# Layer 3's exponentials as a quotient of Sigmoids, and layer 2's h in the order (batch, node)

## The chip, the cores and the metric

The kernel runs on one core of a Trainium2 chip. The core has a matrix engine (TensorE, "PE" in the profile, with "PEld" for its weight loads), a vector engine (VectorE, "DVE"), a scalar engine for functions of one variable (ScalarE, "ACT"), a general engine (GpSimd, "POOL") and a queue for transfers (SyncE, "SP"). They run side by side and wait for each other with semaphores. The metric is the device time of one execution in microseconds (us).

## The reference, cut to what matters

The input x is (128 graphs, 64 nodes, 256 features), fp32, with one 64 x 64 adjacency matrix. Four layers follow one another, each as x = layernorm(x + layer(x)). Layers 0 and 1 (a graph convolution with batch norms, and an attention with an MLP) aren't touched by the change. Layer 2 is two graph convolutions, then four rounds of LSTMs over windows of p nodes; layer 3 is an attention of a graph with itself.

```python
# layer 2, after its convolutions: h is (batch, node, 256)
for p in range(1, 5):
    nw = T // p
    wins = h[:, :nw * p, :].reshape(B * nw, p, H)
    last = lstm_last(Wih[p-1], Whh[p-1], bih[p-1], bhh[p-1], wins)   # p steps over each window
    h = h.at[:, arange(nw) * p + (p - 1), :].set(last.reshape(B, nw, H))

# layer 3
Wh = einsum('bnf,fo->bno', h, W)
e = (Wh @ a1)[:, :, None] + (Wh @ a2)[:, None, :]
e = where(e >= 0, e, 0.2 * e)
e = where(adj == 0, -inf, e)
h_prime = einsum('bij,bjo->bio', softmax(e, -1), Wh)
```

So each round p reads the nodes 0, p, 2p ... as step 0, the nodes 1, p+1, ... as step 1, and so on, and overwrites the last node of each window.

## The kernel before, in words

**Tiles and blocks.** The 128 graphs are cut into 16 blocks of 8 graphs (512 rows of 256 features, four tiles of 128 rows) and into 4 groups of 32 graphs. Work tiles (`mem`) and PSUM tiles (`PS`) are handed out from stocks. Layer 2's h of a group is one SBUF tile `Hg[g]`, features on the partitions, 4096 floats each; `hT[g]` is its view as (partition, half of the features c, node n, graph b). With b last, the 32 graphs of one node are neighbours in memory.

**Order of the work.** Each piece of work is a generator that yields a `step` with an engine and an estimated duration before it issues instructions. `flow` keeps an estimated clock per engine and always continues the generator that could start soonest, so the order of instructions on each engine is fixed when the program is built and follows from the estimates in the `step` calls. A step for ScalarE may name its function table (`tbl="exp"`, `"sigmoid"`, `"gelu"`): a change of table adds 1.3 us to the estimate.

**Layer 2.** `gcn_block` runs the convolutions of one block and the LSTM of p=1, whose result is written into h through `hT_block(i)` (L1357). `unit` runs the windows of p = 2, 3 or 4 over one group: p=2 and p=3 in two units per group (16 and 16, or 12 and 9 windows, times 32 graphs), p=4 in one unit per group for three groups (16 windows, 32 graphs), and in two units of 16 graphs for the last group. `src` is the part of h that a unit reads, `x_of(s, q)` its step s, `out_of` writes the new h (L1389). A unit of 32 graphs is cut into two halves q: by windows where the count of windows is even, by graphs otherwise.

In `lstm`, the gates of step 0 are products with h as the moving operand (L1055). Later steps of a unit in halves take seven products for eight (sums and differences of halves and weights): T1 = x_v - x_u on POOL (L1147), T3 = h_v - x_v on VectorE (L1173), and the products go through `product` (L1127), of which one per gate, A11, has the half x_u of h as its moving operand. The last two units, in one part, use `plain_steps`: products with h (L1264) and with the hidden state (L1266).

**Layer 3.** `last_block(i, t0, nt)` handles a block (the last four blocks in two halves of two tiles). It loads the residual x, copies its part of h to a work tile in the order (graph, node) on ScalarE (L1467), transposes it on TensorE (`to_tm`, L359), adds (L1478), normalises, transposes again (L353), multiplies with W and the two score columns (L1507), builds the scores in PSUM (L1531, L1532), caps and leaks them (L1536, L1538), takes the row maximum (L1539), negates it (L1540), takes one Exp per tile with the sum as a by-product (L1544), divides (L1546, L1547), transposes (L1553), multiplies with Wh (L1563), adds to x (L1574), normalises (L272 to L314) and stores (L1578). The blocks of groups 0 to 2 begin as soon as the last unit of their group has ended; so layer 3's blocks run among the LSTMs of later groups, whose Sigmoids and tanhs are on ScalarE too (L1203 to L1286).

Of the kernel before, what the change touches and what calls it, by code (L numbers as in the profile page):

```python
# [10 lines left out]
AF = mybir.ActivationFunctionType  # L11
ALU = mybir.AluOpType
AX = mybir.AxisListType
PSUM = bass.MemoryType.PSUM

P = 128
B, N, D = 128, 64, 256
# [16 lines left out]
def kernel(ctx: ExitStack, tc: tile.TileContext, a: dict, out: bass.AP):  # L34
    nc = tc.nc
    V, S, G, T = nc.vector, nc.scalar, nc.gpsimd, nc.tensor

    def bc_mid(ap, n):

        return ap.unsqueeze(1).to_broadcast([ap.shape[0], n, ap.shape[1]])  # L40

    def bc_last(ap, n):

        return ap.unsqueeze(2).to_broadcast([ap.shape[0], ap.shape[1], n])

    def tm(s):

        return s.rearrange("p (t d) -> p t d", t=NT)

    def fm(s):  # L50

        return s.rearrange("p (c k) -> p c k", c=2)
# [59 lines left out]
    def mark(*key):  # L112
        done[key] = Clock.end
# [7 lines left out]
    def step(e, us, ps=0, sl=0, waits=True, at=None, tbl=None):  # L121

        return (e, us, ps, sl, waits, at, tbl)
# [83 lines left out]
    def ctile(shape, name, pool=cp):  # L212
        return pool.tile(shape, F32, tag=name, name=name)
# [6 lines left out]
    Hg = [ctile([P, 4 * NT * D], f"h{g}", big) for g in range(NG)]  # L220
    Hs = [Hg[i // 4][:, (i % 4) * NT * D : (i % 4 + 1) * NT * D] for i in range(NBLK)]
    H = [fm(s) for s in Hs]
    hT = [t.rearrange("p (c n b) -> p c n b", c=2, n=N) for t in Hg]
    XD = [dram.tile([P, NT, D], F32, tag=f"xd{i}", name=f"xd{i}") for i in range(NBLK)]

    PS = Stock([ctile([P, NT * D], f"ps{j}", psp) for j in range(4)])
    mem = Stock([ctile([P, NT * D], f"t{j}", big) for j in range(TEMPS)])
# [96 lines left out]
    def joined(ps, n=2 * NT):  # L324

        return ps.rearrange("p (s g e) -> p g s e", s=2, e=N)[:, :n]

    def runs(ap):

        if len(ap.shape) == 2:  # L330
            return ap.rearrange("p (g s e) -> p g s e", s=2, e=N)
        return ap.rearrange("p t (c s e) -> p (t c) s e", s=2, e=N)

    def aggregate(ps, y, mT):


        for c in range(2):
            for t in range(NT):
                for f, to in enumerate(halves):
                    for s, h in enumerate(halves):  # L340
                        T.matmul(  # L341
                            part(ps, s, c * NT + t)[to],
                            y[h, t, c * P + f * N : c * P + (f + 1) * N],
                            mT[h, h],
                            start=True,
                            stop=True,
                        )
# [7 lines left out]
    def to_tm(ps, yT):  # L355

        for t in range(ps.shape[1]):
            for c in range(2):
                T.transpose(ps[:, t, c * P : (c + 1) * P], yT[:, c, t * P : (t + 1) * P], ident)  # L359
# [13 lines left out]
    def mm_tm(ps, yT, w, nk):  # L373

        for t in range(NT):
            for k in range(nk):
                T.matmul(  # L377
                    ps[:, t, :],
                    yT[:, k, t * P : (t + 1) * P],
                    w[:, k, :],  # L380
                    start=(k == 0),
                    stop=(k == nk - 1),
                )

    def by_chunk(ap):
        return ap.rearrange("(k p) m -> p k m", p=P)
# [19 lines left out]
    with c0:  # L406
# [299 lines left out]
        for k, w in zip(("Wc", "Wq", "Wk", "Wv", "Wo", "W1", "W2"), (Wc, Wq, Wk, Wv, Wo, W1, W2)):  # L706
            src = by_chunk(a[f"L1_gnn_{k}"])
# [312 lines left out]

    def hT_block(i):

        return hT[i // 4][:, :, :, (i % 4) * 8 : (i % 4) * 8 + 8]

    def lstm(p, n, parts, x_of, out_of):

# [279 lines left out]
    def gcn_block(i):  # L1306
        yield step("T", 1.15, ps=1, sl=1)
        ps = PS.take()
        s_a = mem.take()
        aggregate(PS[ps], X[i], bdAT)  # L1310
        yield step("Q", 4.0, waits=False)
        nc.sync.dma_start(XD[i], X[i])
        mem.add([Xs[i]], Clock.end, part=("x", i // 2) if i < 8 else None)
        mark("x", i)
        yield step("S", 1.05, ps=-1)
        S.copy(runs(mem[s_a]), joined(PS[ps]))
        PS.give(ps)
        yield step("T", 3.45, ps=1, sl=1)
        ps = PS.take()
        s_h1 = mem.take()  # L1320
        mm_tm(tm(PS[ps]), fm(mem[s_a]), Wg0, 2)
        mem.give(s_a)
        yield step("V", 1.25, ps=-1)
        h1 = tm(mem[s_h1])
        V.tensor_tensor(h1, tm(PS[ps]), bc_mid(rb0, NT), ALU.add)
        PS.give(ps)
        yield step("S", 1.05)
        S.activation(mem[s_h1], mem[s_h1], AF.Relu)
        yield step("T", 1.15, ps=1, sl=1)
        ps = PS.take()  # L1330
        s_a = mem.take()
        aggregate(PS[ps], h1, bdAT)
        mem.give(s_h1)
        yield step("S", 1.05, ps=-1)
        S.copy(runs(mem[s_a]), joined(PS[ps]))
        PS.give(ps)
        yield step("T", 3.45, ps=1, sl=1)
        ps = PS.take()
        s_h2 = mem.take()
        mm_fm(fm(PS[ps]), Wg1, fm(mem[s_a]), 2)  # L1340
        mem.give(s_a)
        yield step("V", 1.4, ps=-1)
        h2 = fm(mem[s_h2])
        for c in range(2):
            V.tensor_tensor(
                h2[:, c, :].rearrange("p (b n) -> p b n", b=8),
                fm(PS[ps])[:, c, :].rearrange("p (b n) -> p b n", b=8),
                bc_mid(rb1[:, c, :], 8),
                ALU.add,
            )  # L1350
        PS.give(ps)
        t = yield step("S", 1.05)
        S.activation(mem[s_h2], mem[s_h2], AF.Relu)  # L1353


        def out_of(q, c, o, th):
            V.tensor_tensor(  # L1357
                hT_block(i)[:, c, :, :].rearrange("p n b -> p b n"), o, th, ALU.mult
            )

        yield step("T", 0.0)
        h2 = h2.rearrange("p c (b n) -> p c b n", b=8)
        yield from lstm(1, TB, [(slice(0, TB), 8)], lambda s, q: h2, out_of)
        yield step("V", 0.0)
        mem.give(s_h2)
        mark("p", 1, i)

    def unit(p, g, w0, nw, b0, nb):
        src = hT[g][:, :, w0 * p : (w0 + nw) * p, b0 : b0 + nb].rearrange("p c (w q) b -> p c w q b", q=p)

        hn = nw * nb // 2
        even = nw % 2 == 0
        parts = [(slice(q * hn, (q + 1) * hn), nw // 2 if even else nw) for q in range(2)]
        if nb < BG:
            parts = [(slice(0, 2 * hn), nw)]

        def half(ap, q):

            if len(parts) == 1:
                return ap  # L1380
            if even:
                return ap[..., q * nw // 2 : (q + 1) * nw // 2, :]
            return ap[..., q * nb // 2 : (q + 1) * nb // 2]

        def x_of(s, q):
            return half(src[:, :, :, s, :], q)

        def out_of(q, c, o, th):
            V.tensor_tensor(half(src[:, c, :, p - 1, :], q), o, th, ALU.mult)  # L1389

        yield from lstm(p, nw * nb, parts, x_of, out_of)
        mark("p", p, g, w0, nw, b0, nb)
# [63 lines left out]
    def last_block(i, t0=0, nt=NT):  # L1456
# [3 lines left out]
        x = tm(mem[s_x])[:, :nt, :]  # L1460
        nc.sync.dma_start(x, XD[i][:, t0 : t0 + nt, :])
        r = nt / NT
        yield step("S", 2.2 * r, sl=1)
        s_h = mem.take()
        hb = fm(mem[s_h])[:, :, : nt * P]
        for c in range(2):
            S.copy(  # L1467
                hb[:, c, :].rearrange("p (b n) -> p b n", n=N),
                hT_block(i)[:, c, :, 2 * t0 : 2 * (t0 + nt)].rearrange("p n b -> p b n"),
            )  # L1470
        yield step("T", 0.9 * r, ps=1)
        ps = PS.take()
        px = tm(PS[ps])[:, :nt, :]
        to_tm(px, hb)
        mem.give(s_h)
        mark("read", i)
        yield step("V", 0.1 + 1.2 * r, ps=-1)
        V.tensor_tensor(x, px, x, ALU.add)  # L1478
# [6 lines left out]
        px = fm(PS[ps])[:, :, : nt * P]  # L1485
# [40 lines left out]
        e, aT, d = (mem[s_e][:, j * nt * N : (j + 1) * nt * N].rearrange("p (t m) -> p t m", t=nt) for j in range(3))  # L1526
# [8 lines left out]
        mx = sm.tile([P, NT], F32, tag="mx3", name="mx3")  # L1535
# [1 line left out]
        PS.give(ps)  # L1537
        V.scalar_tensor_tensor(e, e, 0.2, e, ALU.mult, ALU.max)  # L1538
        V.reduce_max(mx[:, :nt], e, axis=AX.X)  # L1539
        V.tensor_scalar(mx[:, :nt], mx[:, :nt], -1.0, None, ALU.mult)  # L1540
        yield step("S", 0.3 * nt, tbl="exp")
        sums = sm.tile([P, NT], F32, tag="sums3", name="sums3")
        for t in range(nt):
            S.activation(e[:, t, :], e[:, t, :], AF.Exp, bias=mx[:, t : t + 1], accum_out=sums[:, t : t + 1])  # L1544
        yield step("V", 0.3 + 0.3 * r)
        V.reciprocal(sums[:, :nt], sums[:, :nt])  # L1546
        V.tensor_tensor(e, e, bc_last(sums[:, :nt], N), ALU.mult)  # L1547
        yield step("T", 0.1 + 0.5 * r, ps=1)
# [36 lines left out]
    seq, n = [], 0  # L1585
# [85 lines left out]
    def last_of(i, *part):  # L1671
        return (lambda: ready(("wx",), *units_at_end(i)), lambda: last_block(i, *part), 3)
# [66 lines left out]
```

## Time and profile before

| what | value |
|---|---|
| median of 3 runs | 2407.23 us (2405.26 to 2409.41) |
| profiled execution, its own time | 2409.44 us |
| its span in the profile | 2407.7 us |
| busy: PE, DVE, ACT, POOL | 2287.2, 1287.7, 1187.4, 591.7 us |
| granted TensorE clock, mean | 0.982 |
| layer 2's units (L1127 with h) | from about 1340 us |
| layer 3's first copy (L1467) | 1859.6 us |
| last write of h (L1389) | 2372.1 us |

Busy time is the time in which an engine worked on an instruction; matmuls are pipelined, so the mean length of one is more than the distance from one to the next. In a group line, the columns after the bar are busy time in us, mean length of one in ns, and then the idle time of the engine just before these instructions with what ended it. A matmul's name lists the moving operand first and the stationary one second; a tile goes by the name of the memory that it lies in, so "x", "t", "wA" or "rows" can be a work tile in lent memory.

### The profile page before, as it was taken

Reading aid. Unit: us, or ns where it says so; the run is one execution under the profiler, and the core shown is the slowest. Engines: PE = TensorE matmul, PEld = TensorE weight load, DVE = VectorE, ACT = ScalarE, POOL = GpSimd, SP = SyncE. Lnnn points to the kernel's source line nnn. Section 1 sums busy time; section 2 is a strip of 40 time slices with the busy share of each in tenths; the row PEclk is TensorE's granted clock in tenths of the full one; section 3 lists DMA queues with packets and bytes.
Section 4 is the critical chain, followed back from the end, with each engine's and each line's share of the span. In section 5 each row is a group of like instructions: output and inputs, shape, how many; then the busy total and the mean of one; then the engine's idle time right before and its main releaser. Section 6 shows DMA issues by size and latency. Waiting matters only on the chain.

```text
span 2407.7 us, 40603 instructions
## 1 busy us (share of the span) xinstructions
PE 2287.2 (95%) x16916; PEld 1759.9 (73%) x16916; DVE 1287.7 (53%) x2904; ACT 1187.4 (49%) x2189; POOL 591.7 (25%) x441
## 2 busy tenths in 40 slices
PE   8999788999989999999999999999999999998997
PEld 4548665666665666666667788899999888887785
DVE  4557678566483474744643433454444444455546
ACT  2257643544434544335453443444444653468766
POOL 0012134232242232331321222222221222122122
PEclk9999899999999999999999999999999999999998
DMA  6100301000000000001000000000001000001111
GB/s 162 49 1 1 111 23 49 28 10 10 1 12 17 10 10 10 1 10 36 36 19 27 18 1 1 17 2 1 1 1 36 1 10 9 19 27 66 40 36 45
DMA packets 42633, 57.91 MB, mean 24 GB/s; under 512 B 6224, under 2 KB 35536, under 8 KB 42448
## 3 DMA queue, kind: packets, MB, share of 16 engines
q1 hardware_dynamic: 41344, 54.22, 7.0%
q8 instruction: 133, 2.18, 0.4%
q10 hardware_dynamic: 1104, 1.08, 0.1%
q14 instruction: 52, 0.43, 0.1%
HBM read 38.52 MB, written 16.78 MB: 23 GB/s over the span
## 4 chain that ended last, share of the span: by engine, by line
PE 60%; DVE 16%; ACT 7%; POOL 3%; issue 2%; POOLq 0%; ACTq 0%; DVEq 0%
PE ps L1127 26%; PE ps L1055 11%; PE ps L365 7%; PE ps L377 4%; PE ps L938 4%; DVE ln_st L272 3%; ACT x L314 2%; PE ps L808 2%; POOL ln_rs L308 1%; PE ps L1507 1%; DVE x L300 1%; PE ps L341 1%; DVE ln_mv L273 1%; PE ps L353 1%; DVE ln_nm L311 1%
## 5 line engine op out<-in xcount | busy, mean ns | idle before, releaser
L1127 PE MATMUL ps<-x,x 128*128 128x256 f32 x928 | 225.0, 380 | 0.7 <-DVE t L1195 0.7
L1127 PEld LDWEIGHTS ps<-x,x 128*128 128x128 f32 x928 | 173.5, 190 | 24.9 <-issue 1.6
L314 ACT ACTIVATE x<-x,ln_nm,ln_rs 128x256 f32<-128x256 f32 x212 | 112.3, 592 | 133.3 <-DVE ln_nm L311 131.9
L1127 PE MATMUL ps<-t,x 128*128 128x256 f32 x672 | 163.7, 380 | 0.0
L1127 PEld LDWEIGHTS ps<-t,x 128*128 128x128 f32 x672 | 126.4, 190 | 17.1 <-DVE x L1195 0.8
L308 POOL TENSOR_TENSOR ln_rs<-ln_rs,neghalf 128x4 f32<-128x4 f32 (+1 forms) x72 | 71.2, 990 | 212.0 <-DVE ln_rs L274 186.4
L365 PE MATMUL ps<-t,W1T 128*128 128x512 f32 x256 | 117.8, 607 | 0.0
L1055 PE MATMUL ps<-h,wL 128*128 128x192 f32 (+2 forms) x480 | 103.9, 371 | 4.8 <-ACT h L1353 4.8
L272 DVE BATCH_NORM_STATS2 ln_st<-x 128x6 f32<-128x256 f32 x260 | 99.7, 403 | 0.4
L1055 PEld LDWEIGHTS ps<-h,wL 128*128 128x128 f32 x480 | 75.6, 192 | 29.9 <-issue 22.5
L294 POOL TENSOR_TENSOR ln_rs<-ln_rs,neghalf 128x4 f32<-128x4 f32 x32 | 36.9, 1153 | 217.1 <-DVE ln_rs L274 217.0
L1055 PE MATMUL ps<-h,x 128*128 128x256 f32 x384 | 86.7, 380 | 2.2 <-ACT t L1067 1.8
L1067 ACT ACTIVATE t<-ps,bih 128x512 f32<-128x512 f32 (+3 forms) x98 | 57.2, 634 | 55.8 <-PE ps L1055 55.1
L1203 ACT ACTIVATE x<-x,bih 128x512 f32<-128x512 f32 (+2 forms) x69 | 44.6, 648 | 80.3 <-DVE x L1193 80.0
L1186 DVE COPY x<-ps 128x256 f32<-128x256 f32 (+2 forms) x69 | 26.1, 378 | 108.4 <-PE ps L1127 107.6
L365 PEld LDWEIGHTS ps<-t,W1T 128*128 128x128 f32 x256 | 47.6, 195 | 49.6 <-issue 49.5
L365 PE MATMUL ps<-t,wA 128*128 128x512 f32 x160 | 76.8, 626 | 5.5 <-ACT t L784 5.5
L1055 PEld LDWEIGHTS ps<-h,x 128*128 128x128 f32 x384 | 72.6, 190 | 12.9 <-ACT t L1067 2.2
L1186 DVE COPY t<-ps 128x256 f32<-128x256 f32 (+2 forms) x51 | 18.8, 373 | 103.8 <-PE ps L1127 103.5
L1067 ACT ACTIVATE x<-ps,bih 128x512 f32<-128x512 f32 (+3 forms) x86 | 51.5, 650 | 40.6 <-PE ps L1055 40.4
L273 DVE BATCH_NORM_AGGREGATE ln_mv<-ln_st 128x2 f32<-128x6 f32 x448 | 71.3, 167 | 0.0
L1193 DVE TENSOR_TENSOR x<-ps,x 128x512 f32<-128x512 f32 (+2 forms) x69 | 41.4, 602 | 53.0 <-PE ps L1127 43.6
(714 smaller groups left out, 5713.2 us busy)
## 6 DMA issues: line engine op xcount, KB each, us to landing
t<-in_x_dram SPq DMA_DIRECT2D x26, 512.0 KB, 4.3
xd<-x SPq DMA_DIRECT2D x16, 512.0 KB, 2.6
x<-xd SPq DMA_DIRECT2D x8, 512.0 KB, 3.3
out_dram<-x SPq DMA_DIRECT2D x8, 512.0 KB, 2.9
h<-in_x_dram SPq DMA_DIRECT2D x5, 512.0 KB, 5.2
wL<-in_L_gnn_Wih_dram SPq DMA_DIRECT2D x2, 1024.0 KB, 5.0
x<-in_L_gnn_Whh_dram SPq DMA_DIRECT2D x2, 1024.0 KB, 5.4
x<-xd SPq DMA_DIRECT2D x5, 256.0 KB, 2.9
```

Source lines behind the costliest of these rows:

```text
L272: V.bn_stats(st[:, t, :], y[:, t, :])
L273: V.bn_aggr(mv[:, t, :], st[:, t, :])
L308: G.tensor_tensor(rs, rs, neghalf[:, :n], ALU.pow)
L314: S.activation(y[:, t, :], y[:, t, :], AF.Identity, scale=rs[:, t : t + 1], bias=nm[:, t : t + 1])
L365: T.matmul(ps[:, c, :], w[:, k, (off + c) * P : (off + c + 1) * P], yT[:, k, :], start=(k == 0), stop=(k == nk - 1),)
L377: T.matmul(ps[:, t, :], yT[:, k, t * P : (t + 1) * P], w[:, k, :], start=(k == 0), stop=(k == nk - 1),)
L808: T.matmul(pv[r * N : (r + 1) * N, b, :, :], x1T[:, k, b * N : (b + 1) * N], Wv_par[:, k, r, :, :], start=(k == 0), stop=(k == 1),)
L938: T.matmul(tm(PS[ps])[:, t, :], fm(mem[gs[k // 2]])[:, k % 2, t * P : (t + 1) * P], W2[:, k, :], start=(k == 0), stop=(k == 3),)
L1055: T.matmul(spread(fm(PS[ps])[:, j, :n], q), WL[p][0][:, k, m], x_of(0, q)[:, k], start=(k == 0), stop=(k == 1),)
L1067: S.activation(of(sl)[:, j], fm(PS[ps])[:, j, :n], AF.Tanh if g == 2 else AF.Sigmoid, bias=bias(g, c))
L1127: T.matmul(dst, WS[p][name](k, g), y[:, k], start=first and k == 0, stop=k == 1, skip_group_check=not first)
L1186: V.tensor_copy(y[:, 1, :], v[:, 0, :])
```

## The change

`hT` becomes (partition, c, graph b, node n): the 64 nodes of one graph are neighbours, and step s of a unit reads and writes h with a stride of p floats. p=1 writes h in contiguous rows. Units are always halved by graphs. In layer 3 the copy to (graph, node) order goes, and the transposes read h itself. The softmax subtracts the maximum on VectorE, takes two Sigmoids on ScalarE over all tiles of the block at once, of the scores and of their negative, and forms exp(e) = sigmoid(e) / sigmoid(-e) on VectorE with a reciprocal and a product; the row sums become a reduction of their own.

```diff
-    hT = [t.rearrange("p (c n b) -> p c n b", c=2, n=N) for t in Hg]
+    hT = [t.rearrange("p (c b n) -> p c b n", c=2, n=N) for t in Hg]
...
-        return hT[i // 4][:, :, :, (i % 4) * 8 : (i % 4) * 8 + 8]
+        return hT[i // 4][:, :, (i % 4) * 8 : (i % 4) * 8 + 8]
...
-            V.tensor_tensor(
-                hT_block(i)[:, c, :, :].rearrange("p n b -> p b n"), o, th, ALU.mult
-            )
+            V.tensor_tensor(hT_block(i)[:, c], o, th, ALU.mult)
...
     def unit(p, g, w0, nw, b0, nb):
-        src = hT[g][:, :, w0 * p : (w0 + nw) * p, b0 : b0 + nb].rearrange("p c (w q) b -> p c w q b", q=p)
+        src = hT[g][:, :, b0 : b0 + nb, w0 * p : (w0 + nw) * p].rearrange("p c b (w q) -> p c b w q", q=p)
 
         hn = nw * nb // 2
-        even = nw % 2 == 0
-        parts = [(slice(q * hn, (q + 1) * hn), nw // 2 if even else nw) for q in range(2)]
+        parts = [(slice(q * hn, (q + 1) * hn), nb // 2) for q in range(2)]
         if nb < BG:
-            parts = [(slice(0, 2 * hn), nw)]
+            parts = [(slice(0, 2 * hn), nb)]
...
-            if even:
-                return ap[..., q * nw // 2 : (q + 1) * nw // 2, :]
-            return ap[..., q * nb // 2 : (q + 1) * nb // 2]
+            return ap[..., q * nb // 2 : (q + 1) * nb // 2, :]
 
         def x_of(s, q):
-            return half(src[:, :, :, s, :], q)
+            return half(src[..., s], q)
 
         def out_of(q, c, o, th):
-            V.tensor_tensor(half(src[:, c, :, p - 1, :], q), o, th, ALU.mult)
+            V.tensor_tensor(half(src[:, c, :, :, p - 1], q), o, th, ALU.mult)
...
-        yield step("S", 2.2 * r, sl=1)
-        s_h = mem.take()
-        hb = fm(mem[s_h])[:, :, : nt * P]
-        for c in range(2):
-            S.copy(
-                hb[:, c, :].rearrange("p (b n) -> p b n", n=N),
-                hT_block(i)[:, c, :, 2 * t0 : 2 * (t0 + nt)].rearrange("p n b -> p b n"),
-            )
...
-        to_tm(px, hb)
-        mem.give(s_h)
+        to_tm(px, hT_block(i)[:, :, 2 * t0 : 2 * (t0 + nt)].rearrange("p c b n -> p c (b n)"))
...
         V.reduce_max(mx[:, :nt], e, axis=AX.X)
-        V.tensor_scalar(mx[:, :nt], mx[:, :nt], -1.0, None, ALU.mult)
-        yield step("S", 0.3 * nt, tbl="exp")
+        V.tensor_tensor(e, e, bc_last(mx[:, :nt], N), ALU.subtract)
+
+        yield step("S", 0.2 + 0.65 * r, tbl="sigmoid")
+        S.activation(d, e, AF.Sigmoid, scale=-1.0)
+        S.activation(e, e, AF.Sigmoid)
+        yield step("V", 0.4 + 1.0 * r)
         sums = sm.tile([P, NT], F32, tag="sums3", name="sums3")
-        for t in range(nt):
-            S.activation(e[:, t, :], e[:, t, :], AF.Exp, bias=mx[:, t : t + 1], accum_out=sums[:, t : t + 1])
-        yield step("V", 0.3 + 0.3 * r)
+        V.reciprocal(d, d)
+        V.tensor_tensor(e, e, d, ALU.mult)
+        V.reduce_sum(sums[:, :nt], e, axis=AX.X)
         V.reciprocal(sums[:, :nt], sums[:, :nt])
         V.tensor_tensor(e, e, bc_last(sums[:, :nt], N), ALU.mult)
```

## The prediction

> **What bounds the kernel now.** I read the page's totals first, then busy time by stretch, then the lines that touch the changed tile h. Totals and the 40 slices:
>
> ```profile
> span 2407.7 us, 40603 instructions
> PE 2287.2 (95%) x16916; PEld 1759.9 (73%) x16916; DVE 1287.7 (53%) x2904; ACT 1187.4 (49%) x2189; POOL 591.7 (25%) x441
> PE   8999788999989999999999999999999999998997
> ```
>
> TensorE is busy 95% of the span, VectorE and ScalarE about half. Busy time by stretch, in which columns are PE, PEld, DVE, ACT, POOL, then granted clock, shows where that is exact:
>
> ```profile
> 1500.00:1600.00 100.00, 100.00 (x525) 91.00 (x524) 45.99 (x78) 44.51 (x97) 26.22 (x19) 1.00 0.04 11
> 1860.00:2150.00 290.00, 286.45 (x1623) 254.50 (x1623) 133.13 (x310) 151.79 (x347) 68.11 (x53) 1.00 0.03 8
> 2150.00:2372.00 222.00, 204.04 (x1304) 168.65 (x1302) 118.62 (x412) 170.63 (x393) 44.28 (x54) 0.99 0.15 50
> 2372.00:2408.00 36.00, 21.14 (x151) 15.67 (x151) 21.33 (x97) 23.98 (x65) 7.88 (x13) 0.80 0.16 52
> ```
>
> Through layer 2's recurrences (about 1340 to 2150) TensorE never stops: a nanosecond more per column is a nanosecond more of kernel. Idle TensorE where layer 3's blocks run: 3.6 us (1860 to 2150), 18.0 (2150 to 2372), 14.9 (last 36). What layer 3's edits can give is a part of these.
>
> **The products that read h.** Groups by form (busy us, mean ns): the moving operand is named first, h; p=4's weights are wB, p=3's wL, p=2's x.
>
> ```profile
> L1055 PE MATMUL ps<-h,wB 128*128 128x256 f32 x192 | 43.0, 380 | 0.3 <-ACT t L1494 0.3
> L1127 PE MATMUL ps<-h,wB 128*128 128x256 f32 x144 | 37.9, 385 | 0.9 <-ACT t L1207 0.9
> L1264 PE MATMUL ps<-h,wB 128*128 128x256 f32 x192 | 50.4, 385 | 1.9 <-ACT t L1269 1.1 <-DVE x L1478 0.6
> L1055 PE MATMUL ps<-h,wL 128*128 128x192 f32 x192 | 33.3, 327 | 0.0
> L1127 PE MATMUL ps<-h,wL 128*128 128x144 f32 x128 | 21.9, 294 | 1.9 <-ACT h L1207 0.7 <-DVE x L1478 0.7 <-ACT t L1207 0.5
> ```
>
> Each product in the code leaves two records (L1264: 96 products, 192 records). The mean overlaps its neighbours; the pace is the distance of starts. In the timeline (start, length):
>
> ```profile
> 2354.90 1.03 PE L1264 MATMUL ps<-h,wB 128*128 128x256 f32 x4
> 2355.76 1.03 PE L1266 MATMUL ps<-h,x 128*128 128x256 f32 x4
> ```
>
> Four records in 0.86 us: 0.215 us for 256 columns, 0.84 ns per fp32 column, for products that read h (L1264) as for those that read a plain buffer (L1266), because h now lies (node, batch) and is read in runs of 16 or 32 neighbouring floats.
>
> What a bad step costs in this very tile is visible on two other engines. L1467 (ScalarE) reads h with a step of 32 floats; L1357 (VectorE) writes it with that step, L1193 works on contiguous rows:
>
> ```profile
> L1467 ACT COPY x<-h 128x512 f32<-128x512 f32 x10 | 10.4, 1094 | 0.0
> L1467 ACT COPY x<-h 128x256 f32<-128x256 f32 x2 | 1.2, 638 | 0.0
> L1357 DVE TENSOR_TENSOR h<-x,t x8: 1035/1063/2515, 567.0 to 1356.7; 128x512 f32<-128x512 f32 x8
> L1193 DVE TENSOR_TENSOR x<-ps,x 128x512 f32<-128x512 f32 x32 | 22.0, 689 | 26.4 <-PE ps L1127 22.3 <-ACT x L1205 2.0 <-ACT t L1205 1.1
> ```
>
> ScalarE: (1094-638)/256 = 1.78 ns per element. VectorE: 1063 against 689, +0.73 ns on its contiguous 1.04: 1.77. Two engines with different rates meet the same 1.78, so it looks like the memory's, not the engine's.
>
> [...] no row shows steps of 8 to 16 bytes, and none shows TensorE. [...]
>
> **The change, part by part.** *Order of h.* A product of step p now reads the nodes p floats apart: 8 bytes (p=2), 12 (p=3), 16 (p=4). Same number of products, no new wait.
> p=4: 192+144+192 = 528 records. Doubled: 528 x 0.215 = +113 us; at 1.78 ns a column, 256 x 1.78 = 0.456, +0.241 each: +127. Lower end 0. I take +120.
> p=3: [...] 320 records of 192 columns (0.1625 to 0.256: +30) and 320 of 144 (0.1225 to 0.192: +22): upper end +52, lower 0. I take half, +26, because nothing here shows how such a mixture is served.
> p=2: [...] at most +7 on 512 records; I take 0.
> Other accesses of h: L1357 falls from 1.06 to about 0.69 us, 32 of them, -12 us of VectorE, hidden under TensorE (460 to 1360). POOL's L1147 (1.26 us for 512) and VectorE's L1173 and L1389 (0.42 us for 256) get the steps of 8 to 16 bytes, at worst x1.7, some +25 us of POOL and +30 of VectorE. POOL is 25% and VectorE 45% busy there, and L1147 is issued ahead of its use: taken as 0; without that cover a step's stage 1 would wait about 1 us, 33 times.
>
> *The copies in layer 3.* L1467 goes: 24 x 1.09 + 16 x 0.63 = 36 us of ScalarE, and a slot. The transposes read h directly, as weights and contiguous: cost 0.
>
> *The exponentials.* Rows of now:
>
> ```profile
> L1544 ACT ACT_TABLE_LOAD x16 | 20.5, 1283 | 5.5 <-DVE mx L1540 5.3
> L1269 ACT ACT_TABLE_LOAD x10 | 12.8, 1283 | 0.2
> L858 DVE RECIPROCAL sums<-sums 128x16 f32<-128x16 f32 x16 | 4.0, 247 | 0.3
> L1546 DVE RECIPROCAL sums<-sums 128x4 f32<-128x4 f32 x12 | 2.1, 171 | 9.3 <-ACT x L1544 7.7 <-ACT t L1544 1.6
> ```
>
> 31 table loads after 1850 (16 before exp, 15 back) at 1.283: -40 us of ScalarE. Exps 12 x 1.44 + 8 x 0.72 = -23. Two Sigmoids of 256 at about 0.45 (L1269's 0.47 carries a bias), of 128 at 0.33: 12 x 0.9 + 8 x 0.66 = +16. ScalarE in all: -36-40-23+16 = -83 us.
> VectorE: a subtraction of 0.42 for a 0.16 scale, a product of 0.42, a sum of 0.41, and the reciprocal of the full tile. From 16 and 4 elements (247-171)/12 = 6.3 ns each: 256 take 0.15+1.6 = 1.75 us[...]. 12 x (0.26+0.42+0.41+1.75) = 34, half blocks 8 x (0.13+0.28+0.28+0.95) = 13: +47 us.
> The latency of one softmax: before 1.28+1.44 on ScalarE and 0.6 on VectorE, 3.3 us; after 0.26+0.9+3.2 = 4.4. Four blocks run interleaved, so in the middle the load counts, not the latency.
>
> *What the relief gives.* Of the 18 us idle in 2150 to 2372 a part stands directly behind table loads:
>
> ```profile
> 2161.24 1.28 ACT L1203 ACT_TABLE_LOAD   x1
> 2163.69 0.68 PE L1553 MATMUL ps<-ident,t 64*64 64x64 f32 x16 [2.51 <-ACT t L1207]
> ```
>
> With ScalarE from 171 to about 115 of these 222 us and VectorE from 119 to about 145, I give it half: -9 us. Last 36 us: the copies at 2372.6 to 2376.5 go (about -3, since VectorE's additions L1478 queue next), and the four last half blocks put 1.6 us more on VectorE each, about two of them in line at the end (+3): 0. A slower TensorE hides some of the remaining idle: -7.
>
> **Sum**, against the profiled execution's 2409.4 (span 2407.7): +120 +26 -9 -7 = +130, 2539; the median of the runs shown is 2 us lower: 2537.
>
> **Rivals.**
> *TensorE's reads don't mind the step*[...]. For it: no row shows TensorE suffering[...]. Against it: fp32 columns come at 0.84 ns[...]. Then -9 alone, with +-7 for another order out of the planner: 2398, faster. It decides at a pace of L1264: still 0.215 us.
> *The whole line price, 12 and 8 bytes too*: +127+52+7-16 = +170: 2577[...].
> *VectorE becomes the end*: TensorE unharmed, but reciprocals at 1.75 us delay x's additions and statistics, all in order on VectorE behind them, and the tail gains nothing: 18 us idle stay, tail +3 to +6: 2407 to 2413. It decides where VectorE passes about 80% after 2150; I get 65%.
> *The loads stay*: only if another function of a third set ran there; none does after 1345. Under 0.02.
>
> **How the numbers follow.** Slower reads in p=4, with half of p=3, 0.42 (2505 to 2563); the whole line price 0.16 (2563 to 2595); unharmed reads 0.32 (2385 to 2405); VectorE's end 0.10. Slower by over 0.2% (4.8 us, about what a measurement of this kernel can tell from no change): 0.42+0.16+0.04 = 0.62; within 0.05; faster 0.33. The range takes in most of both signs: 2394 to 2585, leaving out about 0.07 below and 0.06 above. The likeliest case's own range is 2505 to 2563.
>
> **What would show it.** In the changed profile: L1264's x products (four records in 1.7 to 1.8 us instead of 0.86) and L1055's wB group, busy time near doubled; p=3's between 1.0 and 1.6 times; p=2's unchanged; no L1467; no table load after layer 1's last; a DVE RECIPROCAL 128x256 near 1.75 us; L1357's successor near 0.69 us; VectorE +47-12 us plus its strided part, ScalarE -83. The prediction is wrong if L1264 keeps 0.215 us, and then the time is 2398; or if strided POOL work delays stage 1.

## The result and the profile after

The changed kernel takes 2587.6 us (median of four runs, 2583.4 to 2587.8) against 2407.2 us: a ratio of 1.0745, 95% interval 1.0726 to 1.0764. The sign of the prediction was right and its size wrong: 2537 was predicted, and 2587.6 lies just above the upper end of its range, 2585.

The page of the changed kernel, totals and the row of slices for TensorE:

```profile
span 2586.1 us, 40497 instructions
PE 2468.7 (95%) x16916; PEld 1805.6 (70%) x16916; DVE 1337.6 (52%) x2964; ACT 1110.0 (43%) x2030; POOL 613.6 (24%) x441
PE   7999689999999999999999999999999999989996
```

There are as many matmul records as before (16916), but they take 181.5 us more (2468.7 - 2287.2), and the span is 178.4 us longer. TensorE's total idle time is almost what it was, 117.4 us against 120.5. ScalarE lost 77.4 us, nearly the 83 predicted.

The groups of the changed kernel with h as moving operand, from 1340 us on (busy us, mean ns of one, idle before):

```profile
L1264 PE MATMUL ps<-h,wB 128*128 128x256 f32 x192 | 95.0, 628 | 0.0
L1055 PE MATMUL ps<-h,wB 128*128 128x256 f32 x192 | 88.1, 630 | 0.0
L1127 PE MATMUL ps<-h,wB 128*128 128x256 f32 x144 | 71.4, 631 | 0.6 <-DVE x L1464 0.4 <-ACT t L1207 0.2
L1055 PE MATMUL ps<-h,x 128*128 128x256 f32 x288 | 64.9, 377 | 0.0
L1055 PE MATMUL ps<-h,wL 128*128 128x192 f32 x192 | 51.9, 429 | 0.0
L1055 PE MATMUL ps<-h,wL 128*128 128x144 f32 x192 | 42.9, 387 | 0.0
L1127 PE MATMUL ps<-h,wL 128*128 128x192 f32 x128 | 38.6, 429 | 0.0
L1127 PE MATMUL ps<-h,wL 128*128 128x144 f32 x128 | 32.6, 384 | 0.1
```

Lines of before that the prediction doesn't show, for p=3 and p=2:

```profile
L1055 PE MATMUL ps<-h,wL 128*128 128x144 f32 x192 | 25.5, 286 | 0.0
L1127 PE MATMUL ps<-h,wL 128*128 128x192 f32 x128 | 26.6, 330 | 0.0
L1055 PE MATMUL ps<-h,x 128*128 128x256 f32 x288 | 64.6, 379 | 0.0
```

Set against before: p=4 (wB), 254.5 - 131.3 = +123.2 us. p=3 (wL), 166.0 - 107.3 = +58.7 us; the two L1055 groups with wL were 33.3 and 25.5 us, the two L1127 groups 26.6 and 21.9. p=2 (x, the step-0 products alone): 64.9 against 64.6, nothing. The three sum to 182.2 and account for all of TensorE's growth. The pace, the distance from start to start, shows it in the timeline of the changed kernel (start, length):

```profile
2500.37 1.04 PE L1266 MATMUL ps<-h,x 128*128 128x256 f32 x4
2501.25 1.97 PE L1264 MATMUL ps<-h,wB 128*128 128x256 f32 x4
2503.04 1.04 PE L1266 MATMUL ps<-h,x 128*128 128x256 f32 x4
```

From L1264's start to the next L1266 it is 1.79 us for four records, 0.448 us each; L1266, which reads a plain buffer, still gives way to the next group after 0.88 us, 0.22 each.

What stays is idle time. I split both kernels at the end of the last write of h; behind it only layer 3 is left, "the tail" from here on. Rows are the stretch, its length, busy time and instructions of PE, PEld, DVE, ACT, POOL, then granted clock (the last two columns are of transfers and aren't used). Before:

```profile
1340.00:2372.52 1032.52, 1009.84 (x5755) 897.92 (x5753) 487.90 (x1143) 551.93 (x1262) 233.29 (x193) 1.00 0.05 18
2372.52:2407.70 35.18, 21.14 (x151) 15.67 (x151) 20.90 (x96) 23.46 (x64) 7.88 (x13) 0.80 0.15 50
```

After, with the write that ends the first stretch:

```profile
L1384 DVE TENSOR_TENSOR h<-rows x1: 619/619/619, 2536.7 to 2536.7; 128x256 f32<-128x256 f32 x1
1340.00:2537.32 1197.32, 1187.30 (x5713) 943.11 (x5715) 533.11 (x1166) 476.54 (x1108) 253.77 (x191) 0.99 0.04 15
2537.32:2586.10 48.78, 25.59 (x196) 17.47 (x196) 35.20 (x135) 21.83 (x56) 10.34 (x15) 0.75 0.13 44
```

Ahead of the last write TensorE's idle time falls from 22.7 to 10.0 us, by 12.7. In the tail it rises from 14.0 to 23.2: 9.1 us go back. 196 matmul records stand in the tail where there were 151, and 35 us of VectorE where there were 21. So 123.2 + 58.7 - 12.7 + 9.1 = +178.3, the growth of the span.

VectorE's and GpSimd's groups in the changed kernel: the reciprocals of whole tiles, the write of h in p=1, which is now contiguous (it was 1063 ns), and the strided T1 of the seven-product steps on GpSimd (it was about 1290; the row mixes p=2 and p=4):

```profile
L1533 DVE RECIPROCAL x<-x 128x256 f32<-128x256 f32 x4 | 7.0, 1744 | 0.3 <-ACT x L1529 0.3
L1533 DVE RECIPROCAL h<-h 128x128 f32<-128x128 f32 x3 | 2.8, 945 | 0.4 <-ACT h L1529 0.4
L1357 DVE TENSOR_TENSOR h<-x,x 128x512 f32<-128x512 f32 x5 | 3.3, 688 | 6.5 <-ACT x L1067 6.5
L1147 POOL TENSOR_TENSOR t<-h 128x512 f32<-128x512 f32 x8 | 16.5, 2065 | 46.6 <-PE ps L1127 27.1 <-PE ps L1553 14.6 <-DVE t L1102 4.6
```

### The profile page after: what moved, and what is told of

It reads as the page before. It is cut to its first block, busy times and chain, and to the rows that moved or that the text cites. A ratio compares the mean times of both kernels' runs of the same rounds, so it can differ in the third digit from the quotient of the medians.

```text
span 2586.1 us, 40497 instructions
## 1 busy us (share of the span) xinstructions
PE 2468.7 (95%) x16916; PEld 1805.6 (70%) x16916; DVE 1337.6 (52%) x2964; ACT 1110.0 (43%) x2030; POOL 613.6 (24%) x441
## 4 chain that ended last, share of the span: by engine, by line
PE 68%; DVE 14%; ACT 3%; POOL 2%; issue 2%; POOLq 0%; ACTq 0%; DVEq 0%
PE ps L1127 26%; PE ps L1055 15%; PE ps L365 7%; PE ps L938 3%; PE ps L1264 3%; PE ps L377 3%; DVE ln_st L272 3%; PE ps L1493 2%; PE ps L1266 2%; PE ps L808 1%; DVE x L300 1%; PE ps L341 1%; PE ps L353 1%; ACT x L314 1%; POOL ln_rs L308 1%
## 5 line engine op out<-in xcount | busy, mean ns | idle before, releaser
L1127 PE MATMUL ps<-t,x 128*128 128x256 f32 x768 | 187.2, 380 | 0.0
L1127 PE MATMUL ps<-x,x 128*128 128x256 f32 x704 | 172.3, 380 | 2.1 <-ACT t L1167 1.4
L1127 PEld LDWEIGHTS ps<-t,x 128*128 128x128 f32 x768 | 144.5, 190 | 28.8 <-issue 10.4
L314 ACT ACTIVATE x<-x,ln_nm,ln_rs 128x256 f32<-128x256 f32 x200 | 106.4, 593 | 135.2 <-DVE ln_nm L311 135.0
L1127 PEld LDWEIGHTS ps<-x,x 128*128 128x128 f32 x704 | 132.2, 190 | 25.8 <-issue 4.6
L1055 PE MATMUL ps<-h,wL 128*128 128x192 f32 (+2 forms) x480 | 138.3, 448 | 4.8 <-ACT h L1353 4.8
L1055 PEld LDWEIGHTS ps<-h,wL 128*128 128x128 f32 x480 | 94.3, 198 | 41.0 <-issue 21.2
L1264 PE MATMUL ps<-h,wB 128*128 128x256 f32 x192 | 95.0, 628 | 0.0
L1055 PE MATMUL ps<-h,x 128*128 128x256 f32 x384 | 88.8, 383 | 2.4 <-ACT t L1067 2.1
L1055 PE MATMUL ps<-h,wB 128*128 128x256 f32 x192 | 88.1, 630 | 0.0
L1055 PEld LDWEIGHTS ps<-h,x 128*128 128x128 f32 x384 | 72.7, 190 | 15.0 <-ACT t L1067 2.5
```

Of the source, the lines that this page charges most:

```text
L314: S.activation(y[:, t, :], y[:, t, :], AF.Identity, scale=rs[:, t : t + 1], bias=nm[:, t : t + 1])
L1055: T.matmul(spread(fm(PS[ps])[:, j, :n], q), WL[p][0][:, k, m], x_of(0, q)[:, k], start=(k == 0), stop=(k == 1),)
L1127: T.matmul(dst, WS[p][name](k, g), y[:, k], start=first and k == 0, stop=k == 1, skip_group_check=not first)
L1264: T.matmul(shaped(dst), WL[p][0][:, k, m], x[:, k], start=(k == 0), stop=False)
```

## The experiments

Two questions: which read pays what (theory, called the line theory in the expectations: the step of the reads is what TensorE pays for, at 16 bytes the 1.78 ns a column that ScalarE and VectorE showed for an element at 128, at 12 bytes less, at 8 next to nothing; what 8 and 12 bytes cost no row of before shows; rival: something else in the new order, such as the strided work on VectorE and GpSimd or another order of instructions), and why the quotient, which frees ScalarE, gives nothing at the end.

**The two parts alone.** The order of h with Exp kept (the softmax lines of before in the changed kernel):

```diff
-        S.activation(d, e, AF.Sigmoid, scale=-1.0)
-        S.activation(e, e, AF.Sigmoid)
...
+        for t in range(nt):
+            S.activation(e[:, t, :], e[:, t, :], AF.Exp, bias=mx[:, t : t + 1], accum_out=sums[:, t : t + 1])
```

> The order (batch, node) alone, with the exponentials of before. If the whole loss is TensorE's reads with a step (the line theory), TensorE's busy time rises by about 181 us as in the changed kernel and the time is 2575 to 2590. If the quotient of Sigmoids has a large share of the loss (its tail was 52 us against 35), the time is 2570 or less.

And the quotient with the old order of h and the copies (those lines the other way round, in the kernel before):

> The quotient of Sigmoids alone, with h in the order (node, batch) and the copies kept. Line theory: TensorE's busy time as before, and only the relief of ScalarE is left: 2390 to 2405. Rival, that the reciprocals on VectorE lengthen the tail by more than the table loads gave: 2407 to 2420, with more than 36 us after the last write of h.

The order alone: 2577.6 us, ratio 1.0704 (1.0688 to 1.072). The quotient alone: 2414.3 us, ratio 1.0024 (1.0013 to 1.0035). Their sum, 169.5 and 6.1 over their runs of before, is within 5 us of the whole, 180.4. The order of h is the loss; the quotient, meant to help, costs a little too. The order alone, split at its last write of h:

```profile
1340.00:2534.53 1194.53, 1184.57 (x5740) 940.08 (x5738) 500.84 (x1141) 521.72 (x1220) 252.24 (x192) 1.00 0.05 15
2534.53:2571.60 37.07, 18.69 (x146) 14.16 (x142) 20.86 (x96) 19.22 (x55) 7.84 (x13) 0.79 0.13 43
```

With Exp and its table loads kept, TensorE already idles only 10.0 us ahead of the last write, as in the changed kernel. So the relief doesn't need the quotient.

**What a step costs TensorE.** The kernel before, followed by a strip of matmuls that read the same h tile with one step after another, 24 records each; then the same with h as the weights, 24 records of 128 columns each:

```diff
+    for st_ in (1, 2, 3, 4, 5, 6, 8, 12, 16):
+        mv_ = scr[:, : 256 * st_].rearrange("p (n s) -> p n s", s=st_)[:, :, 0]
+        for f in range(12):
+            T.matmul(pb, ident, mv_, start=True, stop=True)
+    for st_ in (1, 2, 4, 16, 32):
+        wt_ = scr[:, : 128 * st_].rearrange("p (n s) -> p n s", s=st_)[:, :, 0]
...
```

> The kernel before with a strip of products at its end that read 256 fp32 columns with steps of 1, 2, 3, 4, 5, 6, 8, 12 and 16 floats (12 products each), and then weights with steps of 1, 2, 4, 16 and 32 floats. Line theory[...]: distance of starts per record 0.215 us for steps 1 and 2 (0.228 at most), 0.34 for 3, 0.455 for 4 and all larger. Rival, that only a step of 16 bytes and over counts: 0.215 for 3, 0.43 from 4 on. Rival, that the cost goes on rising with the distance: 8 and 16 clearly over 0.46. For weights no theory; the number is the price of a transpose that reads h with a step of 32.

Busy time by stretch in the strip, each from the first record of a step to the first of the next, so 24 records each (the counts in brackets take in a neighbour or two). As moving operand: steps 1, 2, 3, 4, 8 and 16; then as weights: steps 1, 2 and 4.

```profile
2413.10:2418.28 5.18, 5.18 (x26) 4.56 (x24) 0.00 (x0) 0.00 (x0) 0.00 (x0) 1.00 0.00 0
2418.28:2423.69 5.41, 5.41 (x25) 4.51 (x24) 0.00 (x0) 0.00 (x0) 0.00 (x0) 1.00 0.00 0
2423.69:2431.84 8.15, 8.15 (x26) 4.74 (x24) 0.00 (x0) 0.00 (x0) 0.00 (x0) 1.00 0.00 0
2431.84:2442.71 10.87, 10.87 (x26) 5.00 (x25) 0.00 (x0) 0.00 (x0) 0.00 (x0) 1.00 0.01 2
2464.50:2475.57 11.07, 11.07 (x26) 5.00 (x24) 0.00 (x0) 0.00 (x0) 0.00 (x0) 1.00 0.00 0
2486.30:2496.64 10.34, 10.34 (x25) 4.95 (x24) 0.00 (x0) 0.00 (x0) 0.00 (x0) 1.00 0.01 2
2496.64:2499.34 2.70, 2.70 (x26) 2.70 (x24) 0.00 (x0) 0.00 (x0) 0.00 (x0) 1.00 0.00 0
2499.34:2502.16 2.82, 2.82 (x26) 2.82 (x25) 0.00 (x0) 0.00 (x0) 0.00 (x0) 1.00 0.00 0
2502.16:2507.76 5.60, 5.60 (x26) 5.60 (x25) 0.00 (x0) 0.00 (x0) 0.00 (x0) 1.00 0.00 0
```

Divided by 24: step 1, 0.216 us for 256 columns; step 2, 0.225; step 3, 0.340; step 4, 0.453; and from 5 to 16 between 0.431 and 0.461, without rising. That is 0.84, 0.88, 1.33, 1.77 and 1.68 to 1.80 ns a column. Step 4 is not free and step 2 nearly is. Step 3 costs three quarters of step 4 and step 2 half of it: from 2 to 4 the pace is in proportion to the step, 0.44 ns a column for each float. So the line theory met its numbers (at a step of 16 it was 5% too high), and both rivals missed theirs. As weights, h costs the same: 0.112 us for 128 columns at step 1, 0.118 at 2, and 0.218 to 0.233 at 4 and more.

**The same inside the kernel.** The order of h alone, but with windows made of every 16th node (p=4), or of every 12th or 9th (p=3), so that the reads of that p are runs of neighbours. All instructions, sizes and the tile's order stay. VectorE's and GpSimd's reads and writes of h in that p become runs too, so it is TensorE's busy time that tells the engines apart. Both kernels compute other windows than the reference.

```diff
+        if p == 4:
+            src = hT[g][:, :, b0 : b0 + nb, w0 * p : (w0 + nw) * p].rearrange("p c b (q w) -> p c b w q", q=p)
```

> The kernel with only the new order of h (2577.6 us), in which the windows of p=4 alone are taken as every 16th node instead of 4 neighbours, so that the reads of p=4 are runs of 16 neighbouring elements; as many instructions of the same sizes, but other windows than the reference's, so the numbers computed differ. If the step of 16 bytes is the cost and it is paid by p=4's matmuls alone: 2577.6 - 123 = 2452 to 2462 us, matmuls of 128x256 f32 in p=4 back at about 215 ns for a record. If the order costs by something else (more bytes of h between rows, VectorE's or GpSimd's strided work, the planner's order), less than half of that comes back: above 2515 us.

> The kernel with only the new order of h (2577.6 us), in which the windows of p=3 alone are taken as every 12th or 9th node instead of 3 neighbours, so that the reads of p=3 are runs of 12 or 9 neighbouring elements; as many instructions of the same sizes, but other windows than the reference's, so the numbers computed differ. By the two traces the step of 12 bytes costs p=3 58.7 us: 2516 to 2522 us. If it were the 26 us that the prediction took[...]: 2549 to 2554 us.

With p=4 in runs: 2457.8 us, 119.8 below the order alone. With p=3 in runs: 2522.2 us, 55.4 below. TensorE's busy time falls by 118.1 (from 2463.8) and 57.4, nearly all of it, which leaves little for the other engines. Both are what the two traces had led to expect, and the groups of the treated p are back at their old cost. First p=4 in runs (p=3's wL unchanged at 51.8), then p=3 in runs (p=4's wB unchanged at 94.9):

```profile
PE 2345.7 (95%) x16916; PEld 1797.9 (73%) x16916; DVE 1283.1 (52%) x2904; ACT 1151.6 (47%) x2145; POOL 603.3 (25%) x441
L1055 PE MATMUL ps<-h,wL 128*128 128x192 f32 x192 | 51.8, 429 | 0.0
L1264 PE MATMUL ps<-h,wB 128*128 128x256 f32 x192 | 50.1, 383 | 1.1 <-ACT h L1269 1.1
```

```profile
PE 2406.4 (96%) x16916; PEld 1769.2 (70%) x16916; DVE 1289.1 (51%) x2904; ACT 1151.1 (46%) x2145; POOL 604.7 (24%) x441
L1264 PE MATMUL ps<-h,wB 128*128 128x256 f32 x192 | 94.9, 628 | 0.0
L1055 PE MATMUL ps<-h,wL 128*128 128x192 f32 x192 | 33.2, 327 | 0.6 <-ACT t L1207 0.6
```

119.8 + 55.4 = 175.2, where the order alone costs 169.5: no loss is left for another cause, and without its bad steps the order would gain about 6 us. That sum was worked out from the two; both windows in runs together weren't run.

**Why the quotient gives nothing.** In the quotient alone the last write of h ends at 2365.2 us, 7.3 earlier than before (1.1 of that is an earlier start of layer 2), and the tail is 50.2 us long instead of 35.2:

```profile
2365.23:2415.40 50.17, 28.29 (x175) 19.19 (x175) 33.32 (x131) 23.41 (x59) 9.22 (x14) 0.62 0.13 42
```

First suspect: the reciprocals of whole tiles, in line on VectorE. The quotient alone with its `V.reciprocal(d, d)` left out:

```diff
-        V.reciprocal(d, d)
```

> The quotient alone as in the run with h in its old order, but the division by the Sigmoid of the negative is a product with it: the 20 reciprocals of whole tiles are left out, so the weights of layer 3's attention are not the softmax's. If the reciprocals' 28 us of VectorE stand in the way of TensorE and of the tail, this is 5 to 12 us faster than the quotient with them; if they are hidden, within 2 us of it.

2403.1 us, ratio 0.9982 (0.9975 to 0.9988), 11.2 below the quotient (this kernel's weights are no softmax). The 20 reciprocals, 28.6 us of VectorE (12 x 1.75 + 8 x 0.95), were worth 11 us, about half of it ahead of the last write of h, which ends at 2359.8 us instead of 2365.2, and half in the tail; but 175 records still stand in the tail, and it is still 44.3 us long. How much of the tail's half is the reciprocals' own time is not separated: in these two profiles the granted clock in the tail was 0.62 with them and 0.76 without, and TensorE took 28.3 and 23.7 us for as many records. Next, Exp again in the four last blocks, which are worked in halves and fill the tail (`if nt < NT:` the lines of before, else the quotient):

> The kernel before with the quotient in the whole blocks of layer 3 alone; the half blocks, which are worked last, keep Exp for each tile. Theory: the quotient gains about 7 us ahead of the last write of h (loads of the table gone from the stretch where TensorE is full) and loses 15 us behind it (reciprocals in line on VectorE in the tail). With Exp back in the half blocks the tail should fall from 50 us to 35 to 41 us and the last write of h stay at 2365 us, so 2399 to 2408 us, 7 to 14 us below the quotient everywhere (2414.3). Rival: the loss is spread over the whole of layer 3 (longer VectorE work in every block, planner's order), then the tail stays over 45 us and the time over 2410 us.

2413.2 us, ratio 1.0022 (1.0014 to 1.003); 176 records in a tail of 48.3 us. My theory missed: without any quotient in the half blocks the tail is almost as long. Next, the planner's estimate for the VectorE step set to the real duration:

```diff
-        yield step("V", 0.4 + 1.0 * r)
+        yield step("V", 0.5 + 2.7 * r)
```

> The quotient in every block, in the old order of h, with the planner's estimate for its VectorE step set to what the trace shows (0.5 + 2.7 r us in place of 0.4 + 1.0 r). Rival theory, that the 15 us of longer tail come from a wrong order because the planner took the step for too short: 2400 to 2408 us. Theory, that they come from the duration of the reciprocals themselves in a tail where each block waits for VectorE: 2412 to 2416 us, as without the correction.

2414.0 us, ratio 1.0026 (1.0015 to 1.0037), 178 records, 49.9 us: no gain. And no quotient at all, one Exp over all tiles:

```diff
-        V.tensor_scalar(mx[:, :nt], mx[:, :nt], -1.0, None, ALU.mult)
-        yield step("S", 0.3 * nt, tbl="exp")
...
+        V.tensor_tensor(e, e, bc_last(mx[:, :nt], N), ALU.subtract)
+        yield step("S", 0.2 + 0.35 * r, tbl="exp")
+        S.activation(e, e, AF.Exp)
+        yield step("V", 0.4 + 0.9 * r)
...
+        V.reduce_sum(sums[:, :nt], e, axis=AX.X)
```

> The kernel before with one Exp over all tiles of a block after a subtract of the maximum, and a sum on VectorE; no quotient, no reciprocal of the whole tile, the loads of the table stay. If the table loads are what the quotient gains from, the last write of h comes at 2370 to 2373 us, as before; the tail loses 4 to 8 short instructions of ScalarE and gains a subtract and a sum of 0.3 to 0.4 us on VectorE: 2400 to 2410 us. If the gain comes from the many short Exp on ScalarE and not from the loads, the last write of h comes at 2364 to 2367 us and the time is 2398 to 2403 us.

2414.7 us, ratio 1.003 (1.0019 to 1.0042): slower, against both expectations, with 180 records in a tail of 45.7 us. What these five have in common is the subtraction and the sum on VectorE (in the half-blocks variant in the whole blocks alone), and changed `step` estimates. So three kernels keep the work and get the old estimates back, in the quotient alone, in the changed kernel, and (from 0.2 + 0.35 r and 0.4 + 0.9 r) in the one with a single Exp:

```diff
-        yield step("S", 0.2 + 0.65 * r, tbl="sigmoid")
+        yield step("S", 0.3 * nt, tbl="exp")
...
-        yield step("V", 0.4 + 1.0 * r)
+        yield step("V", 0.3 + 0.3 * r)
```

> The quotient in every block, in the old order of h, with the planner told the price and the table of the steps of before (0.3 nt us on ScalarE with Exp's table, 0.3 + 0.3 r us on VectorE), so that it writes out the order of before or nearly so; the work is the quotient's. In every variant with another softmax so far more of layer 3 stood behind the last write of h (175 to 180 matmul records against 151) and the tail was 44 to 50 us against 35. Theory, that the new prices moved layer 3's work behind layer 2 and so lengthened the tail: about 151 records and 36 to 42 us of tail, 2400 to 2408 us. Rival, that the quotient's work itself stretches the tail: over 46 us of tail, 2411 to 2416 us.

> The changed kernel with the planner told the price and the table of the steps of before; work and order of h are the changed kernel's. Theory of the prices: the 10 us that the changed kernel (2587.6) stands above the new order of h alone (2577.6) go, 2574 to 2580 us. Rival, the work of the quotient: 2584 to 2589 us.

> The kernel with one Exp over all tiles of a block (2414.7 us with its own prices), with the planner told the price of the steps of before. Theory of the prices: 2398 to 2406 us, a tail of 34 to 38 us. If one Exp stays at 2412 to 2416 us, its longer VectorE work (a subtract and a sum, 0.3 to 0.4 us each) is the cost and not the order.

| work | new estimates | old estimates | records and length of the tail, new to old | profile, from L1345 (see below) to the end, new to old |
|---|---|---|---|---|
| changed kernel | 2587.6 | 2578.2 (ratio 1.0712, 1.0697 to 1.0726) | 196, 48.8 us to 150, 40.3 us | 2139.5 to 2133.7 us |
| quotient alone | 2414.3 | 2411.4 (1.0013, 1.0007 to 1.002) | 175, 50.2 us to 151, 39.5 us | 1970.1 to 1964.9 us |
| one Exp | 2414.7 | 2407.0 (0.9997, 0.9989 to 1.0005) | 180, 45.7 us to 151, 35.8 us | 1970.1 to 1962.5 us |

Tail rows of the changed kernel and of the quotient alone, each with the old estimates:

```profile
2534.13:2574.40 40.27, 20.15 (x150) 14.54 (x142) 25.29 (x109) 17.97 (x46) 7.86 (x13) 0.78 0.12 40
```

```profile
2367.13:2406.60 39.47, 23.25 (x151) 16.33 (x151) 25.85 (x109) 21.77 (x55) 8.16 (x13) 0.74 0.13 44
```

In all three the records in the tail go back to 150 or 151, and the tails shorten by 8.5 to 10.7 us. The time of the changed kernel fell into the range of the theory. That of the quotient alone lies in the range of the rival, though its tail and its records are those of the theory; one Exp came out 1 us above the theory's range.

The last column takes out what lies ahead of the change: it counts from the first start in this row of L1345, which is in layer 2's convolutions. The changed kernel, then the same with the old estimates:

```profile
L1345 DVE TENSOR_TENSOR h<-ps,rb x8: 678/680/691, 446.6 to 766.8; 128x512 f32<-128x512 f32 x8
L1345 DVE TENSOR_TENSOR h<-ps,rb x8: 679/683/691, 440.7 to 761.1; 128x512 f32<-128x512 f32 x8
```

The second profile is 5.9 us ahead at a point that the change can't have touched: TensorE's records follow in the same order in both until about 2030 us. So two profiled executions can differ by that much without any cause in the edit. (The kernel before and the changed kernel are level there, 446.4 and 446.6 us, so the sums above stand.) Counted from there, the old estimates gain 5.8, 5.2 and 7.6 us; by the medians it is 9.4, 2.9 and 7.7. With the old estimates the changed kernel then stands 3.0 us above the order alone (2130.7 us) and the quotient alone 3.6 above before (1961.3). So the estimates are the larger part of the changed kernel's 10 us over the order alone; that they are all of it, as the medians by themselves say (2578.2 against 2577.6), the profiles don't bear out. The 3 to 4 us that are left fit VectorE's longer work in the tail (25.9 us against 20.9 for the quotient alone), though no run with the old estimates and without the reciprocals separates it. One Exp ends level with before. No variant that does the whole work beat the kernel before by more than the measurement can tell.

Which of the old estimates matters stays open (ScalarE's 1.2 us, the table's 1.3, or VectorE's 0.6); that VectorE's was too short is not the reason, as the run with its real duration shows.

## Why the prediction was wrong, step by step

**p=4, taken as +120 from 528 records: +123.2.** Right, and at the right price: TensorE pays 1.77 ns a column at a step of 16 bytes, as ScalarE and VectorE did an element at a step of 128 bytes (1.78 and 1.77). The rival that TensorE's reads don't mind the step missed: in the strip 256 columns take 0.453 us at a step of 4 floats, where they take 0.216 in a row and 0.225 at a step of 2.

**p=3, taken as half of its upper end, +26: +58.7.** This is the step that failed, and 33 us of the 48 us missed in the span's growth (178.3 against 130). The upper end, 1.33 ns a column, stood on no row of before, and it was the right price: the strip shows 1.33. Halving it had no source. It averaged "no harm" and "full harm", where p=4's own reasoning had already chosen between the two. The reading without the halving stood among the rivals as the whole line price, at 2577, with 0.16 for its chance; it was the nearest, though not with the 7 us for p=2.

The upper end itself was 7 us short (+52 for 58.7), and all of that is in the shorter rows. The timeline of the changed kernel, 16 records of each size with what follows them:

```profile
1663.29 4.32 PE L1055 MATMUL ps<-h,wL 128*128 128x192 f32 x16
1667.45 1.02 PE L1127 MATMUL ps<-h,wL 128*128 128x144 f32 x4
1682.79 3.57 PE L1055 MATMUL ps<-h,wL 128*128 128x144 f32 x16
1686.19 0.82 PE L1127 MATMUL ps<-x,Wg 128*128 128x192 f32 x4
```

192 columns, in rows of 12 nodes, take 0.260 us, where 0.256 was worked out; 144 columns, in rows of 9 nodes, take 0.213, where it was 0.192. Why rows of 9 cost more is not shown.

**p=2, taken as 0: +0.3.** Right, on the 288 records that the row names.

**Relief, -9 and -7: -12.7** ahead of the last write of h. The sum came out near, but by luck in part: the order alone has the same 10.0 us of idle time with Exp and its loads in place, so the softmax, which the -9 counted on, can't be credited with it. It comes with the slower TensorE and with the copies gone, which no run separates.

**Tail, taken as 0: +9.1.** The second failed step, and a smaller one. I weighed the tail's instructions (three copies less, two reciprocals more) but not how many blocks would stand in it. With the changed estimates 45 more matmul records of layer 3 stand behind the last write, where a block's steps wait for one another; with the old ones it is 150 records, and 20.1 us idle for 23.2. The chain of the last blocks and TensorE's wait in the changed kernel:

```profile
2569.46 0.85 DVE t L1533
2572.63 0.84 DVE t L1533
```

```profile
2571.88 0.69 PE L1543 MATMUL ps<-ident,t 64*64 64x64 f32 x8 [5.61 <-DVE t L1537]
```

The reciprocal was sized rightly (1.744 and 0.945 us against 1.75 and 0.95), ScalarE lost 77 us for 83, and the loads of the table are gone. The strided work on GpSimd grew by a factor of 1.6 (2.07 us for about 1.29; 1.7 was allowed for) and stayed hidden, as predicted: TensorE idles 10.0 us in the whole 1197 us from 1340 to the last write.

**VectorE becomes the end, loads stay, unharmed reads:** in the changed kernel VectorE is busy 52% of the stretch from 2150 us to the last write (202.3 of 387.3 us), far from the 80% that the first named as its sign. Of the 31 loads of a table from 1345 us on before (1.283 us each) none is left, and before none stood among the Sigmoids and tanhs from 1345 us to layer 3's first Exp at 1945 us. The first rival's idea wasn't empty, though: with TensorE's reads unharmed, in the quotient alone, the time is 2414.3, a little above its 2407 to 2413, and the reciprocals are worth 11 us. Unharmed reads were to be decided by L1264's pace, and that went to 0.448.

## What to carry to other kernels

Where TensorE is the bound, its moving operand deserves the contiguous side of a layout, even if another engine must then copy: here 36 us of ScalarE copies, which cost the kernel perhaps 6 us, if the gain in the sum above is theirs, saved 175 us. Price a stride at what the engine was measured to take for that step (here, on TensorE, 0.88, 1.33 and 1.77 ns a column at 2, 3 and 4 floats), and don't average a mechanism with its absence. Where estimates decide the order, an edit to an estimate is an edit to the schedule: count the work behind the last producer, before and after, and try the new work once with the old estimates. Before two profiles are compared to a few microseconds, see whether they are level at a point ahead of the edit.

## What the runs showed of the hardware

In the strip an fp32 column read by TensorE takes 0.84 ns in a row, 0.88 at a step of 2 floats, 1.33 at 3 and 1.77 at 4. From there to a step of 16 floats it doesn't rise with the distance (0.431 to 0.461 us for 256 columns, 1.68 to 1.80 ns a column). Weights are read at nearly the same price: 0.112 us for 128 columns in a row, 0.118 at a step of 2, 0.233 at 4. The strip was executed once.
